# A new order of sparse edge items, panel lists and zeros issued elsewhere, and row additions on TensorE in the first group

## The chip, the cores and the metric

The kernel runs on one core of a Trainium2 chip. Its time is the device time of one execution in microseconds (us); several executions are made, and the median is what counts. One further execution is recorded by the hardware profiler: it gives the page and the trace that are read here.

The engines have short names: PE is TensorE (matrix products; PEld its weight loads), DVE is VectorE, ACT is ScalarE, POOL is GpSimd, SP is SyncE, which here only issues DMA transfers. Each engine works through its own queue of instructions in order.

## The reference

The input x has 32 samples of 512 nodes with 256 features; `adj` is a 512x512 matrix, the same for all samples, with about 1.5% of its entries and the whole diagonal not zero. Four layers follow each other.

```python
def gnn(h, A):                                   # layers 0 and 3
    pre_u, pre_v = h @ W1[:d], h @ W1[d:]
    hidden = relu(pre_u[:, :, None, :] + pre_v[:, None, :, :] + b1)
    S = sigmoid(hidden @ W2 + b2)                # one score for each pair (u, v)
    a = einsum('buv,bud->bvd', S * A, h)
    m = einsum('uv,bud->bvd', A, h) * h
    return beta1 * h + beta2 * (a @ Wa + ba) + beta3 * (m @ Wm + bm)

def layer1(z): return z + relu((A @ z) @ W.T + b)
def layer2(y):                                   # attention over the 512 nodes
    feats = y @ W1.T
    f = feats @ W2 + b2
    return softmax(leaky_relu(f[:, None] + f[None, :]) + A) @ feats + bias2 + y
```

A score S is multiplied by A, so it is needed only where A is not zero.

## The kernel before

**Groups and streams.** The 32 samples are worked in eight groups of four (NB = 4). For each group two "edge groups" exist, g0 for layer 0 and g3 for layer 3. Each of them goes through the same pieces:

- `pre` (L570–L582) computes the rows pre_u and pre_v of all nodes and writes them to a table in DRAM, one row of 1024 values (four samples) for each node and kind;
- `edges` (L611) makes the scores of the entries that are not zero;
- `load` (L727) reads the finished score matrix of four samples back into four tiles called SA, two from each half;
- for layer 0 `middle` follows (layer 0's sums, layers 1 and 2, the `pre` of layer 3), for layer 3 `last` (its sums and the output).

**Items.** An edge group has 36 items of 128 entries each. A node's first eight entries make "own" items (`item_of(c, k)`, eight for each of the four chunks c of 128 nodes); what is left over is packed in four "panels" (`panel_of(half, q)`, two for each half of the nodes). For each item `edges` does this: gather 128 rows of the table by an index list on POOL (`fetch`, L607, an indirect DMA of 512 KB); add the rows `mine` of the other end of the edges (L686, DVE; for an own item these are one contiguous load for each chunk by SP, L647, for a panel another gather by POOL); take relu and multiply by W2 (L694 for all four samples at once, or L702 for one sample with the sum); add up each sample's 256 products on ACT (L672). Four items at a time then go through exp and the sigmoid, and `put` scatters each item's 128 x 4 scores to DRAM (L601, POOL, an indirect DMA). Two DRAM tensors called cells, one for each half (chunks 0 and 1 with the panels of half 0; chunks 2 and 3 with those of half 1), take them. A put waits until the earlier one to the same tensor has landed; `put` therefore takes, from the scores that are ready, one of the half that the last put did not use.

**The order of the items** is the list `order` (L232–L240), the same for all sixteen edge groups. Before, it is four of chunk 0, then three runs of eight that alternate between the chunks 0 and 2, 2 and 1, 1 and 3, and at last the four left of chunk 3 with the four panels between them. So the first four items are all of half 0. In the last eight, six are of half 1 and two, the first two panels, are of half 0.

**Order of instructions.** All these are generators ("streams"). `weave` takes their pieces by given times and issues them in that order; a scheduler then fixes each engine's queue. `behind` keeps edge work on DVE and ACT behind the middle stage's newest piece. Fetches run three items ahead of the additions (LEAD, five in the first g0 and the last g3, LEAD_AT_ENDS). The tiles that they land in are five in rotation, and at the two ends a few more: spare tiles that lie in rooms of the middle stage which are free at that moment (`tags`, `spare`).

**The start.** `setup` and `build` (L249) work out from `adj` which entries there are: for each chunk index list, cell addresses and values; after all four chunks the panels (L345–L380), for which POOL gathers four tiles `got` from a DRAM tensor `lists`. They lie in the rooms h1, hT1, mhT0 and hWa0. The cells of both layers, 2 x 4 MB, are filled with zeros by SP (L538): those of layer 0 by `setup`, those of layer 3 by `zeros_behind`, both from one zero tile in the room hWa3. `middle_before` does for the four samples of the first group what needs no score: it loads the turned sample hT (L816–L820, room hT1, one tile for all four in turn) and makes hWa (hT by Wa, 16 instructions) and mhT (sample by adj, 16 instructions in two pieces, times hT on DVE, L750). The matrix products of `mm` all have line L45. Group 1's `first` (its `pre`) is woven between them.

**The end.** In the last group `last_before` does the same for layer 3, with one hT tile for four samples, and `last_behind` waits for SA and makes the sums (`sums`, L1001 and L1010) and the output.

An fp32 matrix product shows in the trace as two instructions of PE.

## Time and profile before

| what | value |
|---|---|
| median of three executions | 3121.13 us (3118.40, 3121.13, 3138.08) |
| profiled execution | 3102.14 us, of it the span 3100.4 us |
| granted TensorE clock, mean | 0.941 |
| busy: PE, DVE, ACT, POOL | 88%, 74%, 43%, 49% |
| data moved by DMA | 679.40 MB, mean 219 GB/s |
| first matrix product of the first middle stage after its SA landed | 268.22 us |
| last SA tile landed | about 3051 us |

The profiled execution was shorter than the median, so a sum is made against its own time. The span runs from the first to the last instruction; busy time is the share of it in which an engine worked. A wait is put down to the event that ended it: "PE pst L45 <- DMA hT<-xT" is time in which PE stood before a product on line 45 until a transfer into hT had landed. The chain that ended last goes back from the last instruction to what let it start, and so on; a piece of it is on the path that sets the time. A transfer called "SA<-cells" goes from the DRAM tensor cells to the tile SA.

### The profile page before, as it was taken

The page shows a single profiled execution, that of the slowest core. Times are in us where ns is not written, and L with a number is a line of the kernel's source. Part 1 is how long each engine was busy: PE and PEld are TensorE (multiplying, and loading weights), DVE is VectorE, ACT ScalarE, POOL GpSimd, SP SyncE. Part 2 cuts the span into 40 slices and gives each one's busy share as a digit, 9 for nine tenths or more (in the row PEclk, how much of TensorE's full clock was granted, in tenths as well). Part 3 has the DMA queues.
Part 4 walks back from the last instruction along what each step waited for, and adds up shares of the span by engine and source line. Part 5 has one row for each costly group of instructions (what it writes and reads, how often), then busy time and mean ns, then how long its engine had stood idle before and what let it go on. Part 6 is the DMA issues. An engine that isn't in the chain of part 4 may idle for free.

```text
span 3100.4 us, 32465 instructions
## 1 busy us (share of the span) xinstructions
PE 2714.6 (88%) x8645; PEld 1642.5 (53%) x8646; DVE 2302.8 (74%) x6026; ACT 1337.8 (43%) x4101; POOL 1522.5 (49%) x1312
## 2 busy tenths in 40 slices
PE   6366888889998999989998999989999899889957
PEld 3133444446654565546664565545664566545636
DVE  6783886889589875989589885888679795772761
ACT  3453554445345433545354442545335343453440
POOL 1462453556346563556346562565436563450561
PEclk9688988999999999999999999999999999999978
DMA  8874556786677766786668766787568766551753
GB/s 285 282 236 152 180 174 225 237 268 213 223 224 263 235 210 219 247 282 213 227 213 258 238 197 213 242 267 237 188 216 268 251 221 208 178 174 58 234 195 115
DMA packets 302719, 679.40 MB, mean 219 GB/s; under 512 B 52672, under 2 KB 170944, under 8 KB 294336
## 3 DMA queue, kind: packets, MB, share of 16 engines
q0 software_dynamic: 120384, 406.01, 41.0%
q1 hardware_dynamic: 163184, 234.01, 22.5%
q10 hardware_dynamic: 18960, 37.24, 3.2%
q8 instruction: 70, 1.15, 0.2%
q14 instruction: 121, 0.99, 0.1%
HBM read 531.12 MB, written 146.01 MB: 218 GB/s over the span
## 4 chain that ended last, share of the span: by engine, by line
PE 51%; DVE 18%; DMA 17%; issue 6%; ACT 4%; POOL 3%; SPq 0%; POOLq 0%; ACTq 0%; DVEq 0%
PE pst L45 24%; PE pst L1001 7%; DVE rows L686 6%; DMA table<-puv 5%; DMA rows<-table,iv 5%; PE pst L570 3%; DVE rows L702 3%; PE pst L861 3%; PE pst L1010 3%; PE pst L572 3%; DMA cells<-s,cell 3%; DVE rows L694 3%; PE pst L883 2%; PE pst L840 2%; DMA SA<-cells 2%
## 5 line engine op out<-in xcount | busy, mean ns | idle before, releaser
L601 POOL DMA_INDIRECT cells<-s,cell x576 | 691.1, 1200 | 740.7 <-DMA cells<-s,cell 370.3
L607 POOL DMA_INDIRECT rows<-table,iv x554 | 663.3, 1197 | 672.7 <-DMA table<-puv 148.1
L686 DVE TENSOR_TENSOR rows<-rows,mine 128x1024 f32<-128x1024 f32 x554 | 670.8, 1219 | 164.7 <-DMA rows<-table,iv 148.8
L672 ACT ACTIVATE rows<-rows 128x256 f32<-128x256 f32 x1096 | 442.9, 407 | 516.7 <-DVE rows L694 511.1
L45 PE MATMUL pst<-adj,h 128*128 128x512 f32 x1024 | 451.3, 592 | 0.3 <-PE pst L941 0.3
L702 DVE SCALAR_TENSOR_TENSOR rows<-rows,L_gnn_W2bc 128x256 f32<-128x256 f32 x1120 | 415.9, 419 | 1.8
L45 PE MATMUL pst<-L_gnn_Wa,hT 128*128 128x256 f32 x1024 | 264.3, 410 | 118.6 <-DMA hT<-xT 64.6
L694 DVE SCALAR_TENSOR_TENSOR rows<-rows,L_gnn_W2bc 128x1024 f32<-128x1024 f32 x274 | 332.3, 1216 | 0.3
L45 PEld LDWEIGHTS pst<-adj,h 128*128 128x128 f32 x1024 | 192.8, 190 | 222.4 <-issue 218.4
L45 PEld LDWEIGHTS pst<-L_gnn_Wa,hT 128*128 128x128 f32 x1024 | 207.7, 208 | 165.8 <-issue 53.1
L45 PE MATMUL pst<-eT,feats 128*128 128x512 f32 x512 | 231.5, 606 | 12.4 <-ACT eT L953 12.4
L45 PE MATMUL pst<-adjT,zW 128*128 128x512 f32 x512 | 227.8, 597 | 6.2 <-ACT zW L865 6.2
L1001 PEld LDWEIGHTS pst<-hWa,SA 128*128 128x128 f32 x896 | 213.7, 328 | 7.7 <-issue 4.5
L1001 PE MATMUL pst<-hWa,SA 128*128 128x256 f32 x896 | 216.8, 398 | 0.0
L861 PE MATMUL pst<-WT,hT 128*128 128x256 f32 x512 | 150.3, 459 | 75.9 <-DVE hT L848 75.9
L672 ACT ACTIVATION_READ_ACCUMULATOR rows<-rows 128x1 f32 x1096 | 206.7, 189 | 0.0
L809 ACT COPY flat<-SA 128x512 f32<-128x512 f32 x128 | 137.6, 1128 | 155.0 <-PE pst L45 60.1
L840 PE MATMUL pst<-flat,hWa 128*128 128x512 f32 x448 | 196.8, 592 | 0.0
L861 PEld LDWEIGHTS pst<-WT,hT 128*128 128x128 f32 x512 | 118.0, 235 | 114.9 <-DVE hT L848 88.1
L575 ACT COPY puv<-pst 128x256 f32<-128x256 f32 x256 | 93.7, 370 | 183.8 <-DVE puv L574 168.1
L574 DVE TENSOR_TENSOR puv<-pst,bc_L_gnn_b 128x256 f32<-128x256 f32 x256 | 105.0, 416 | 90.3 <-DMA table<-puv 53.8
L45 PEld LDWEIGHTS pst<-eT,feats 128*128 128x128 f32 x512 | 97.5, 193 | 127.5 <-issue 109.8
(170 smaller groups left out, 3979.3 us busy)
## 6 DMA issues: line engine op xcount, KB each, us to landing
table<-puv SPq DMA_DIRECT2D x256, 256.0 KB, 5.5
SA<-cells POOLq DMA_DIRECT2D x64, 1024.0 KB, 7.0
h<-in_x_dram SPq DMA_DIRECT2D x64, 512.0 KB, 6.4
mine<-table SPq DMA_DIRECT2D x64, 512.0 KB, 5.3
hT<-xT SPq DMA_DIRECT2D x36, 512.0 KB, 5.1
h<-x2s SPq DMA_DIRECT2D x36, 512.0 KB, 4.1
xT<-hT ACTq DMA_DIRECT2D x32, 512.0 KB, 5.5
x2T<-yT SPq DMA_DIRECT2D x32, 512.0 KB, 5.3
```

The costliest lines, as they stand in the source:

```text
L45: nc.tensor.matmul(out, lhsT, rhs, start=(n == 0), stop=(n == len(pairs) - 1))
L574: nc.vector.tensor_tensor(puv[:, 0, :], pp[:, 0:D], w["b1bc"], ALU.add)
L601: self.nc.gpsimd.indirect_dma_start(out=g.cells[half], out_offset=bass.IndirectOffsetOnAxis(ap=at, axis=0), in_=s, in_offset=None)
L607: self.nc.gpsimd.indirect_dma_start(out=rows, out_offset=None, in_=g.table, in_offset=bass.IndirectOffsetOnAxis(ap=at, axis=0))
L672: self.behind(nc.scalar.activation(part, part, AF.Identity, accum_out=g.s[:, k, b : b + 1]))
L686: self.behind(nc.vector.tensor_tensor(rows, rows, other, ALU.add))
L694: nc.vector.scalar_tensor_tensor(by_entry, by_entry, 0.0, w2, ALU.max, ALU.mult)
L702: nc.vector.scalar_tensor_tensor(part, part, 0.0, w["W2bc"], ALU.max, ALU.mult, accum_out=at)
L809: self.nc.scalar.copy(flat[:, r, :], SA[r][:, :, b])
L840: nc.tensor.matmul(pz, hWa[:, r, cs], flat[:, r, :], start=(r == 0), stop=False)
L861: nc.tensor.matmul(pw[:, at], zT[:, d, cs], m.WT_1[:, d, :], start=(d + k == 0), stop=(d * k == 1))
L1001: nc.tensor.matmul(pz[:, k * D : (k + 1) * D], SA[r][:, cs, b], hWa[:, r, :], start=(r + k == 0), stop=False)
```

## The change

Six things are edited. Line numbers with "after" are those of the changed kernel.

1. The list `order`: two items of chunk 0; six pairs of chunks 0 and 2; two pairs of chunks 1 and 2; six pairs of chunks 1 and 3, with the panels of half 1 behind the first and the fourth pair; and two pairs, each an item of chunk 3 and a panel of half 0. It holds for all edge groups.
2. In `build` the panel counts and the four gathers into `got` come between the chunks 2 and 1 instead of after all chunks; two of the tiles now lie in the room eT, the others in h1 and hT1. The comparisons that read them stay at the end.
3. `zeros` is issued by POOL instead of SP, for both layers; ahead of those of layer 3, DVE sets the zero tile to zero once more, kept behind the middle stage's newest piece.
4. `edges` has a step `hold` at item 5, which gathers the `mine` rows of the panels early into spare rooms: in the first g0 three of the four (rooms eT for two, mhT3), in the last g3 all four (eT for two, hWa0, mhT0). The spare row tiles of the first g0 are three (yT, mhT0, hWa0) instead of two (yT, mhT3).
5. In the first g0 (`on_pe`) every second item, 18 of 36, has its rows and `mine` added by PE: products with the identity matrix, both into one PSUM tile of 512 columns, twice for an item; relu and W2 are then two DVE operations on 512 columns that read PSUM (after L727) instead of L686 and L694.
6. In `last_before` the hT of the samples 1 to 3 lie in rooms of SA3 tiles instead of in the one hT tile.

Put in the order in which the engines get them, POOL now issues the zeros of layer 0 first, then `got`, then the fetches; before, `got` stood behind the first puts. On PE the products of item 19 stand ahead of the first adj piece of `middle_before` for sample 0, those of 21 between its two adj pieces, those of 23 to 33 ahead of one piece each of the samples 1 to 3, and those of 35 behind all. At the seam from g3 to the next g0 the order on POOL (c30, c31: puts to the halves of layer 3; r0: fetch for layer 0; S30, S31: SA loads) changes like this:

```
before  c31 c30 c31 c30 r0 r0 c30 c31 r0 c30 c31 r0 r0 c31 S30 r0 c31 S30 c31 c31 r0 r0 S31 r0 S31
after   c31 c30 c31 c31 r0 r0 c30 c31 r0 c30 c31 r0 c30 r0 c31 c30 r0 c31 S30 S30 S31 r0 r0 S31 r0
```

```diff
@@ -229,14 +229,19 @@
         self.value = pool.tile([P, ITEMS], F32, name="value")
         self.inode = pool.tile([P, 2 * PANELS], I32, name="inode")
 
-        order = [item_of(0, j) for j in range(OWN // 2)]
-        for lead, other in ((0, 2), (2, 1), (1, 3)):
-            for j in range(OWN // 2):
-                order += [item_of(lead, OWN // 2 + j), item_of(other, j)]
-        tail = [panel_of(h, q) for h in range(2) for q in range(PANELS)]
-        for j in range(OWN // 2):
-            order.append(item_of(3, OWN // 2 + j))
-            order += tail[j : j + 1]
+        ends, most = OWN // 4, OWN - OWN // 4
+        order = [item_of(0, j) for j in range(ends)]
+        for j in range(most):
+            order += [item_of(0, ends + j), item_of(2, j)]
+        for j in range(ends):
+            order += [item_of(1, j), item_of(2, most + j)]
+        for j in range(most):
+            order += [item_of(1, ends + j), item_of(3, j)]
+            if j % (most // PANELS) == 0:
+                order.append(panel_of(1, j // (most // PANELS)))
+        for j in range(ends):
+            order += [item_of(3, most + j), panel_of(0, j)]
+        assert len(order) == len(set(order)) == ITEMS
         self.order = order
 
     def value_of(self, j):
@@ -314,6 +319,36 @@
             yield
         acc, v, there, t = (sheet(NC * OWN) for _ in range(4))
         for c in (0, 2, 1, 3):
+            if c == 1:
+
+                pu = psum()[:, 0 : 2 * PANELS]
+                ones_bf = bf2[:, 1024:1025]
+                nc.vector.memset(ones_bf, 1.0)
+                for k in range(2 * PANELS):
+                    h, q = divmod(k, PANELS)
+                    mm(nc, pu[:, k : k + 1], [(full[:, h * 2 + c, q * P : (q + 1) * P], ones_bf) for c in range(2)])
...
+                inode = self.inode
+                nc.vector.tensor_copy(inode, node)
+                nc.vector.tensor_scalar(self.iu, node, 2.0, None, ALU.mult)
...
+                yield
+                gots = []
+                two = tmp.tile([P, 2, 2 * N], F32, name="got", tag="eT")
+                for k in range(2 * PANELS):
+                    if k < 2:
+                        gots.append(two[:, k, :])
+                    else:
+                        gots.append(tmp.tile([P, 2 * N], F32, name=f"got{k}", tag=("h1", "hT1")[k - 2]))
+                    index = bass.IndirectOffsetOnAxis(ap=inode[:, k : k + 1], axis=0)
+                    nc.gpsimd.indirect_dma_start(out=gots[k], out_offset=None, in_=lists, in_offset=index)
+                yield
             at = slice(c, c + 1)
             js = slice(c * OWN, (c + 1) * OWN)
             target, bias = sheet(OWN), sheet(OWN)
@@ -341,42 +376,16 @@
             nc.vector.tensor_scalar(v[:, js], acc[:, js], 0.5, float(N // 2), ALU.mult, ALU.add)
             self.slots(js, v, there, t, row[:, at], spare)
             yield
-        js = slice(NC * OWN, ITEMS)
...
-        gots = []
-        for k in range(2 * PANELS):
-            gots.append(tmp.tile([P, 2 * N], F32, name=f"got{k}", tag=("h1", "hT1", "mhT0", "hWa0")[k]))
-            index = bass.IndirectOffsetOnAxis(ap=inode[:, k : k + 1], axis=0)
-            nc.gpsimd.indirect_dma_start(out=gots[k], out_offset=None, in_=lists, in_offset=index)
-        yield
         for k in range(2 * PANELS):
             at = slice(k, k + 1)
             rank, adj = gots[k][:, 0:N], gots[k][:, N:]
             junk = bf2[:, 2048 + k % 2 * N :][:, 0:N]
             nc.vector.scalar_tensor_tensor(
-                junk, rank, t[:, at], adj, ALU.is_equal, ALU.mult, accum_out=self.value_of(NC * OWN + k)
+                junk, rank, tp[:, at], adj, ALU.is_equal, ALU.mult, accum_out=self.value_of(NC * OWN + k)
             )
-            nc.vector.scalar_tensor_tensor(junk, rank, slot[:, at], ones, ALU.is_le, ALU.mult, accum_out=v[:, at])
-            yield
-        self.slots(js, v, there, t, start, sp, 0)
+            nc.vector.scalar_tensor_tensor(junk, rank, slot[:, at], ones, ALU.is_le, ALU.mult, accum_out=vp[:, at])
+            yield
+        self.slots(slice(NC * OWN, ITEMS), vp, therep, tp, start, sp, 0)
         yield
 
     def slots(self, js, v, there, t, start, spare, off=None):
@@ -528,6 +537,7 @@
             yield
 
     def zeros_behind(self):
+        self.behind(self.nc.vector.memset(self.zero, 0.0))
         self.zeros(self.cells["3"])
         yield
 
@@ -535,7 +545,7 @@
         for c in cells:
             flat = c[0:CELLS, :].rearrange("(q p a) b -> q p (a b)", q=4, p=P)
             for q in range(4):
-                self.nc.sync.dma_start(flat[q], self.zero)
+                self.nc.gpsimd.dma_start(flat[q], self.zero)
 
     def setup_behind(self):
 
@@ -608,7 +618,9 @@
             out=rows, out_offset=None, in_=g.table, in_offset=bass.IndirectOffsetOnAxis(ap=at, axis=0)
         )
 
-    def edges(self, g, spare=()):
+    def edges(self, g, spare=(), panels=(), on_pe=False):
+
+
 
 
 
@@ -618,7 +630,7 @@
         ready, fetched = [], {}
         lead = LEAD_AT_ENDS if spare else LEAD
         tags = [None] * 5 + list(spare)
-        mine = {}
+        mine, held = {}, {}
         places = g.table.rearrange("(c p k) n -> c k p n", p=P, k=2)
 
         def own_1():
@@ -641,7 +653,9 @@
         def fetch(n):
             j = e.order[n]
             c = j // OWN
-            if c >= NC or c not in mine:
+            if j in held:
+                t = held.pop(j)
+            elif c >= NC or c not in mine:
                 t = self.gath.tile([P, GROUP], F32, name="mine", bufs=3)
                 if c < NC:
                     nc.sync.dma_start(t, places[c, 0])
@@ -657,6 +671,17 @@
             self.fetch(rows, g, e.iv[:, j : j + 1])
             fetched[n] = rows, t
 
+        def hold():
+
+            js = [j for j in e.order if j >= NC * OWN]
+            for tag in panels:
+                n = 2 if tag == "eT" else 1
+                t = self.act.tile([P, n, GROUP], F32, name="held", tag=tag)
+                for k in range(n):
+                    j = js.pop(0)
+                    held[j] = t[:, k, :]
+                    self.fetch(held[j], g, e.iu[:, j - NC * OWN : j - NC * OWN + 1])
+
         def put():
 
             at = next((n for n, r in enumerate(ready) if r[0] != self.half), 0)
@@ -682,8 +707,12 @@
         for k in range(ITEMS):
             for _ in range(2 if spare and len(ready) > 2 else 1):
                 put()
+            if k == LEAD_AT_ENDS:
+                hold()
             rows, other = fetched.pop(k)
-            self.behind(nc.vector.tensor_tensor(rows, rows, other, ALU.add))
+            by_pe = on_pe and k % 2 == 1
+            if not by_pe:
+                self.behind(nc.vector.tensor_tensor(rows, rows, other, ALU.add))
             if k + lead < ITEMS:
                 fetch(k + lead)
             if summed:
@@ -691,7 +720,15 @@
             if spare or k % 2 == 1 and k < ITEMS - 3:
                 by_entry = rows.rearrange("p (b d) -> p b d", b=NB)
                 w2 = w["W2bc"].unsqueeze(1).to_broadcast([P, NB, D])
-                nc.vector.scalar_tensor_tensor(by_entry, by_entry, 0.0, w2, ALU.max, ALU.mult)
+                if by_pe:
+                    for b in range(0, NB, 2):
+                        total, at = self.psum(), slice(b * D, (b + 2) * D)
+                        mm(nc, total, [(self.m.ident, rows[:, at]), (self.m.ident, other[:, at])])
+                        nc.vector.scalar_tensor_tensor(
+                            by_entry[:, b : b + 2, :], by_two(total), 0.0, w2[:, 0:2, :], ALU.max, ALU.mult
+                        )
+                else:
+                    nc.vector.scalar_tensor_tensor(by_entry, by_entry, 0.0, w2, ALU.max, ALU.mult)
                 summed.append(lambda k=k, rows=rows: sums(k, rows))
                 if spare:
                     summed.pop(0)()
@@ -957,8 +994,9 @@
         self.nc.sync.dma_start(h, self.x2s[i])
         return h
 
-    def x2T_of(self, i):
-        hT = self.act.tile([P, DC, N], F32, name="hT3", tag="hT")
+    def x2T_of(self, i, hT=None):
+        if hT is None:
+            hT = self.act.tile([P, DC, N], F32, name="hT3", tag="hT")
         self.nc.sync.dma_start(hT, self.x2T[i])
         return hT
 
@@ -966,7 +1004,8 @@
 
         self.ends = []
         for b in range(NB):
-            h, hT = self.x2_of(i + b), self.x2T_of(i + b)
+            room = self.big(F32, 2048, 3)[:, 0 : DC * N].rearrange("p (c n) -> p c n", c=DC) if b else None
+            h, hT = self.x2_of(i + b), self.x2T_of(i + b, room)
             both = self.big(F32, 2048, 0).rearrange("p (k n) -> p k n", k=2)
             hWa = both[:, 0, :].rearrange("p (c d) -> p c d", c=NC)
             mhT = both[:, 1, :].rearrange("p (c n) -> p c n", c=DC)
@@ -1111,9 +1150,9 @@
             behind = end + 0.29, end + 0.45
         streams += [
             (sp.first(g0, t * NB), first, "fill"),
-            (sp.edges(g0, ("yT", "mhT3") if t == 0 else ()), edges0, ""),
+            (sp.edges(g0, *((("yT", "mhT0", "hWa0"), ("eT", "mhT3"), True) if t == 0 else ())), edges0, ""),
             (sp.middle(g0, g3, t * NB), spread(middle_shares(t == 0), start, end), "main"),
-            (sp.edges(g3, ("yT", "h1", "hT1") if t == last else ()), edges3, "free"),
+            (sp.edges(g3, *((("yT", "h1", "hT1"), ("eT", "hWa0", "mhT0")) if t == last else ())), edges3, "free"),
         ]
         if t == 0:
             streams.append((sp.middle_before(g0, 0), spread(AHEAD, -0.15, -0.03), ""))
```

More of the change, by code (lines that the diff above doesn't have):

```diff
@@ L316, in build @@
         for c in (0, 2, 1, 3):
+            if c == 1:
[5 more added lines that the diff above has]
+                    mm(nc, pu[:, k : k + 1], [(full[:, h * 2 + c, q * P : (q + 1) * P], ones_bf) for c in range(2)])
+                u, node, slot, start, sp, vp, therep, tp = (sheet(2 * PANELS) for _ in range(8))
+                nc.vector.tensor_scalar(u, pu, float(HALF - 1), None, ALU.min)
+                nc.vector.tensor_copy(node, u)
+                nc.vector.tensor_scalar(node[:, PANELS:], u[:, PANELS:], float(HALF), None, ALU.add)
+                inode = self.inode
+                nc.vector.tensor_copy(inode, node)
+                nc.vector.tensor_scalar(self.iu, node, 2.0, None, ALU.mult)
+                nc.gpsimd.iota(slot, [[0, 2], [P, PANELS]], 0, 1, allow_small_or_imprecise_dtypes=True)
+                nc.vector.tensor_scalar(start, u, float(N), None, ALU.mult)
+                nc.vector.tensor_scalar(sp, slot, float(CELLS + NC // 2 * OWN * P), None, ALU.add)
+                nc.vector.tensor_scalar(tp, slot, 1.0, None, ALU.add)
+                yield
[9 more added lines that the diff above has]
+                yield
             at = slice(c, c + 1)
@@ L343, in build @@
             yield
-        js = slice(NC * OWN, ITEMS)
-        pu = psum()[:, 0 : 2 * PANELS]
-        ones_bf = bf2[:, 1024:1025]
-        nc.vector.memset(ones_bf, 1.0)
-        for k in range(2 * PANELS):
-            h, q = divmod(k, PANELS)
-            mm(nc, pu[:, k : k + 1], [(full[:, h * 2 + c, q * P : (q + 1) * P], ones_bf) for c in range(2)])
-        u, node, slot, start, sp, v, there, t = (sheet(2 * PANELS) for _ in range(8))
-        nc.vector.tensor_scalar(u, pu, float(HALF - 1), None, ALU.min)
-        nc.vector.tensor_copy(node, u)
-        nc.vector.tensor_scalar(node[:, PANELS:], u[:, PANELS:], float(HALF), None, ALU.add)
-        inode = self.inode
-        nc.vector.tensor_copy(inode, node)
-        nc.vector.tensor_scalar(self.iu, node, 2.0, None, ALU.mult)
-        nc.gpsimd.iota(slot, [[0, 2], [P, PANELS]], 0, 1, allow_small_or_imprecise_dtypes=True)
-        nc.vector.tensor_scalar(start, u, float(N), None, ALU.mult)
-        nc.vector.tensor_scalar(sp, slot, float(CELLS + NC // 2 * OWN * P), None, ALU.add)
-        nc.vector.tensor_scalar(t, slot, 1.0, None, ALU.add)
-        yield
-        gots = []
-        for k in range(2 * PANELS):
-            gots.append(tmp.tile([P, 2 * N], F32, name=f"got{k}", tag=("h1", "hT1", "mhT0", "hWa0")[k]))
-            index = bass.IndirectOffsetOnAxis(ap=inode[:, k : k + 1], axis=0)
-            nc.gpsimd.indirect_dma_start(out=gots[k], out_offset=None, in_=lists, in_offset=index)
-        yield
         for k in range(2 * PANELS):
```

## The prediction

> **What bounds the kernel now.** First the page: busy time and the costliest groups.
>
> ```profile
> PE 2714.6 (88%) x8645; PEld 1642.5 (53%) x8646; DVE 2302.8 (74%) x6026; ACT 1337.8 (43%) x4101; POOL 1522.5 (49%) x1312
> ...
> L601 POOL DMA_INDIRECT cells<-s,cell x576 | 691.1, 1200 | 740.7 <-DMA cells<-s,cell 370.3
> L607 POOL DMA_INDIRECT rows<-table,iv x554 | 663.3, 1197 | 672.7 <-DMA table<-puv 148.1
> L686 DVE TENSOR_TENSOR rows<-rows,mine 128x1024 f32<-128x1024 f32 x554 | 670.8, 1219 | 164.7 <-DMA rows<-table,iv 148.8
> ```
>
> TensorE is busy 88% of the span, so it is nearly the bound; what an edit can win lies in the other 12%. Every put (L601) and every fetch (L607) holds POOL 1.2 us, and puts to one half wait for each other: 370.3 us of POOL's idle time is that. Next, where TensorE's idle time lies: busy time by stretches (start in three pieces, first middle stage, the steady groups, the end).
>
> ```profile
> 140.00:200.00 60.00, 24.77 (x70) 15.39 (x71) 52.15 (x94) 30.61 (x135) 41.35 (x32) 0.68 0.72 236
> 200.00:268.00 68.00, 38.92 (x97) 20.30 (x95) 29.45 (x55) 24.83 (x98) 36.97 (x35) 0.84 0.77 266
> 268.00:482.00 214.00, 178.48 (x509) 95.36 (x510) 152.59 (x405) 105.60 (x279) 85.70 (x75) 0.88 0.48 152
> 482.00:2880.00 2398.00, 2235.81 (x7178) 1348.27 (x7177) 1858.32 (x5030) 1045.96 (x3080) 1217.63 (x1040) 0.97 0.69 223
> ```
>
> The columns are PE, PEld, DVE, ACT, POOL, granted clock, DMA share, GB/s. Steady groups: PE 2235.8 of 2398, 93%. From 140 to 268 it is 64 of 128, at a clock of 0.68 and 0.84, while DVE has 52 of the first 60. What PE waits for there, in the waits of 0 to 268:
>
> ```profile
> PE pst L45 <- DMA hT<-xT: 64.6, 3, 37.3
> ...
> DVE big L374 <- DMA got<-lists,inode: 16.0, 1, 16.0
> ```
>
> and the chain that ended last, of that stage (start, length, what):
>
> ```profile
> 138.15 4.26 DMA got<-lists,inode
> ...
> 149.31 7.20 DMA hT<-xT
> ...
> 254.72 6.84 DMA cells<-s,cell
> 262.08 4.98 DMA SA<-cells
> 267.08 1.10 ACT flat L809
> 268.22 2.08 PE pst L840 x2
> ```
>
> So the first middle stage starts at 268.22, behind the last puts and the SA load of the first group. Two strands lead there: POOL and DVE (fetch, add, put), and PE's four rounds of middle_before, each behind a load into the one hT tile (149.31, 185.64, 209.22, 235.49), the last done at 252.4. Then the waits from 400 to 2700:
>
> ```profile
> POOL cells L601 <- DMA cells<-s,cell: 309.0, 137, 6.1
> ...
> DVE rows L686 <- DMA rows<-table,iv: 117.5, 42, 8.8
> ...
> PE pst L861 <- DVE hT L848: 71.1, 18, 8.5
> ```
>
> The third is what the first costs at the seams g3→g0: fetches stand on POOL behind puts of one half in a row (1003.75, 1010.08, 1016.35, 1021.70), rows come late, DVE stops for up to 8.8 us, and L848, queued behind the add, holds PE. Last, the end of the chain:
>
> ```profile
> 3028.96 12.12 PE pst L45 x32
> 3041.07 0.46 PE pst L1001 x2
> 3041.53 0.44 issue
> 3041.98 0.56 POOL SA L727
> 3042.54 8.43 DMA SA<-cells
> 3051.02 8.57 PE pst L1001 x26
> ```
>
> The last SA tile lands at 3051, behind half-1 puts at 3027.20, 3030.50, 3035.32 and 3039.33; after it 49 us of sums remain.
>
> **The start (lists, spare rooms, TensorE's adds).** *Lists.* The four list gathers no longer stand behind the first puts on POOL, and their adds lie before chunks 1 and 3 of the build. DVE's 16.0 us at 142.44 go. What is late next: the first rounds of fetches. Fetches begin at 83.13, a put and a fetch take 1.2 + 0.3 us each, and 36 + 36 + 4 of them are 114 us; POOL could be through at 197 and is at 258, so it isn't POOL's rate but the round DVE–ACT–put. DVE has 52.15 of 60 us in 140–200. The 16 us count at most once, as the earlier first hT load: the got tiles hold h1 and hT1 until about 149. I take 7 of them (0 to 16), so a first load at 142: SP's loads of that moment and the build's own DVE work stay in front.
> *Held panel rows, three spare row tiles.* Four panel fetches move ahead of item 10's (4 × 1.5 = 6 us of POOL, same count); one more row tile lets a fetch start earlier. I cost both at nothing while DVE, 52 of 60 us busy, is behind the fetches; if that cover goes, 6 us either way, inside the bounds below.
> *Adds on TensorE.* 18 odd items leave an add (L686, pitch 1.14 us) and a 128x1024 product (L694, 1.14) and get two 128x512 products out of PSUM; no such row exists, nearest are L750 and L930, 0.60 us at a pitch: 18 × (2.28 − 1.20) = 19 us off DVE. PE gets 18 × 4 fp32 matmuls of 128x512. Nearest row: L45 with adj, eight in 6.87–7.03 us, 0.86 each: 72 × 0.86 = 62 us. Upper end: a row from behind a wait, L45 on hT at 156.64, takes 3.75 us for what takes 1.89 at 163.42, so every group that starts cold takes up to twice as long: 62 to 124. PE has 13.2 + 9.2 + 24.8 + 38.9 = 86 us of the 188 from 80 to 268; it has room for 62, not for 124.
> But the items' matmuls stand in PE's in-order queue between the pieces of middle_before (items 19, 21, 23 … 33 each ahead of one piece, 35 after all). An item whose rows are late holds the next round, and what is queued behind it is group 1's pre and the hT of the next sample. A round is then: hT load 7, PE's own hWa (16 instructions, 3.45–5.24) and adj (16, 7.03), two items 6.9, pre 2.6, and the turn over DVE's L750: about 29 us, where it was 36, 24 and 26. From a load at 142, 4 × 29 = 116: PE ends at 258 instead of 252.4. Item 35 still has product (1.2), sums (1.7), sigmoid (2), put (1.2, landing 3–5) and SA load (5–7) behind it, about 15–20 us. SA at 273–278 against 267, +8.
> *Zeros out of the window.* 4 MB of the 8 MB of zeros leave the stretch 40–110, which runs at 325–390 GB/s with DMA full (share 0.91–1.02): 4 MB at 390 GB/s is 10.8 us of DMA; part of it was filling gaps, so −4 (−8 to 0).
> Sum of the start: +8 for PE's rounds, less 4, less 2 for DVE's lighter queue: **+2** (−20, if the whole 16 us and 4 of the zeros count; +20, if the items start cold).
>
> The Trainium skill, "TensorE: Matmul & The Clock Gate", section "What's actually happening", says the clock has two states, half and full, and that some 3.4 us of work set it full. The 3.75 against 1.89 us above is such a factor of two. By it the items would partly pay for themselves: in the 37, 19, 8 and 9 us in which PE waits for hT they keep the clock up, and the hWa groups of four rounds would take 3.45 instead of 5.24 us, 7 us in all.
>
> **Zeros for layer 3.** They go from SP's queue to POOL's, behind a DVE memset inside the first middle stage. POOL: 8 issues at 0.57 (L727's row) + 0.3 = 7 us, ahead of the first c00 puts and fetches; 4 MB of DMA at 390 GB/s is 11 us, where DMA share is 0.48. SP loses eight issues that hold it 12.93 us at 23.86, where the zeros for layer 0 move to POOL too, and are out earlier. DVE's memset of 128x1024 about 1 us. Cover: PE has 178.5 of 214 in that stretch and edge work is not late until the g0→g3 seam. **+3** (0 to +8, all of it if the fetches behind them are late).
> The Trainium skill, "DMA: Bandwidth & Descriptors", section "Issuing engine by pattern", gives simple loads and stores to SyncE, and says POOL's path is the slower. By its first-byte figures, 1 us against 0.6, eight issues in a row would be 0.4 us later; the trace's own landing times (7.3 us median for zeros from SP) don't tell the paths apart.
>
> **The order of items, steady groups.** At the seam g3→g0 the old end is eight items of half 1 with the panels; now the last eight alternate halves. POOL's order there holds two half-1 puts fewer in series ahead of the r0 fetches, but one SA load of half 1 (which waits for the last put) moves ahead of three of them. Two puts are 2 × 5 us off each seam; the SA wait takes about 5 back on half of the fetches. Seven seams have 117.5/7 = 17 us of DVE waits each and 71.1/7 = 10 of PE. If a seam gives PE 1.5 us, seven give 10: **−10** (−40, over half of the 71.1; +10, if the SA wait holds the fetches). At the seam g0→g3 the c00 put moves behind half 1, S00 with it; nothing there waits over 3 us.
>
> **The end.** The two early panel rows and the last puts alternate halves: of the four half-1 puts 3.3–5.0 us apart, two become half-0 puts which overlap. Held panel rows remove `mine<-table,iu` at 3004.48, 8.06 us in the chain, but its fetch joins an earlier POOL queue. hT rooms take 19.6 + 15.0 + 6.2 us of PE waits on x2T off a strand that ends at 3041, before SA; they hide behind SA, and new: three SA3 tiles wait until those rooms are read. −10 (−18, the half-1 puts and the panel's 8 us both; −3, only one put): **−10**.
>
> **Sum.** +2 + 3 − 10 − 10 = −15 on the profiled execution's 3102.14 (span 3100.4, 2 us around it). That execution is 19 us below the median of 3121.13; I put the difference on the median: **3106**. Low ends: −20 + 0 − 40 − 18 = −78; high ends: +20 + 8 + 10 − 3 = +35. 1%, 31 us, is about what a measurement of this kernel (3118 to 3138) tells from no change.
>
> **Rivals.**
> *The seams pay in full (0.25).* For it: PE's 71.1 us at seams come from one cause, and the got stall of 16 us is a plain wait. Start −12, zeros +2, seams −30, end −13: −53, 3068. Against: POOL's waits move to the SA load.
> *TensorE's queue holds the start (0.22), slower.* One mechanism: middle_before's hT loads stand behind items whose rows are late. It decides once an item's wait is longer than PE's idle time in that round (8–9 us in the last two). Three items late by 7 us: start +22, zeros +5, seams 0, end −5: +22, 3143; with cold items (+20 more) 3163.
> *Nothing moves (0.08).* The puts' landing times set seams and end in any order: 3121.
> The forecast itself 0.45, 3088 to 3120.
>
> Faster by over 1%: the first rival but its weak third, and the forecast's low edge: 0.17 + 0.09 = 0.26. Slower by over 1%: half of the second: 0.12. Within 1%: 0.62. The range leaves out the far half of each outer rival: 3062 to 3148.
>
> **What the profile after would show.** Right: no DVE wait on got; the first hT load at 140–145; DVE waits on PE at the new product; first L840 at 265–280; DVE's waits on rows between 400 and 2700 below 90 us and PE's on L848 below 60; last SA tile 8–12 us earlier against the end. Wrong, if the first L840 comes after 285 or before 250, if the seams' waits stay at 117 and 71, or if SA's load at the end waits for PE's reads of the rooms.

## The result, and the profile after

The changed kernel takes 3182.34 us (median of four executions, 3179.11 to 3184.80), the kernel before beside it 3128.21 us (3118.40 to 3138.08): a ratio of 1.017, with a 95% interval of 1.015 to 1.019. It is 54 us slower. The forecast was 3106 us, 15 us faster, with a range up to 3148: sign and range were both wrong.

One caution about the profiles. The profiled execution of the kernel before took 3102.14 us, while none of its timed executions in the studies below was under 3114; their medians were 3128 to 3132. The two profiled spans differ by 3177.2 − 3100.4 = 77 us, the medians by 54. So some 23 us of what the two traces show, most of it in the steady groups, belongs to that one quick execution. Sizes below come from medians; traces are used for where and why.

From the page of the changed kernel, its busy times and the lines that answer to those shown of before:

```profile
PE 2788.7 (88%) x8789; PEld 1669.3 (53%) x8790; DVE 2286.9 (72%) x6027; ACT 1338.6 (42%) x4101; POOL 1529.1 (48%) x1328
...
L611 POOL DMA_INDIRECT cells<-s,cell x576 | 696.5, 1209 | 708.3 <-DVE s L648 298.0
L617 POOL DMA_INDIRECT rows<-table,iv x552 | 664.9, 1204 | 719.5 <-DMA table<-puv 277.4
L715 DVE TENSOR_TENSOR rows<-rows,mine 128x1024 f32<-128x1024 f32 x537 | 648.3, 1217 | 242.6 <-DMA rows<-table,iv 193.9
```

What was to be moved is moved: PE is busy 74 us longer, DVE 16 us shorter, and DVE has 17 additions fewer in the trace. But the wait of the puts now ends at DVE (L648 makes the scores), no longer at the put before; and DVE's idle time ahead of the additions rose from 164.7 to 242.6 us.

Busy time by stretches (PE, PEld, DVE, ACT, POOL, granted clock, DMA share, GB/s), with the start up to the first middle stage, that stage, and the steady groups:

```profile
140.00:200.00 60.00, 41.87 (x109) 22.67 (x108) 36.80 (x66) 30.81 (x138) 33.46 (x29) 0.83 0.71 234
200.00:284.90 84.90, 54.22 (x130) 27.21 (x128) 19.55 (x49) 18.86 (x68) 22.77 (x25) 0.83 0.42 129
284.90:509.00 224.10, 185.33 (x515) 97.58 (x516) 153.46 (x406) 107.74 (x280) 88.91 (x83) 0.86 0.53 173
509.00:2972.00 2463.00, 2248.18 (x7175) 1349.44 (x7174) 1857.11 (x5028) 1043.92 (x3078) 1225.22 (x1040) 0.96 0.68 217
```

In the second stretch no engine is near its limit: PE 54 of 85, DVE 20, POOL 23, DMA share 0.42. The start is now a chain of waits between engines. The steady stretch has nearly the same PE work as before (2248 us against 2236) in a longer time (2463 us against 2398).

Where the time went can be dated by the first score product (L840, after it L877) of each sample in the timeline. Sample 1 of the first group came at 320.3 and now at 341.4, 21 us later; the last of the 32 samples at 2818.6 and now at 2911.2, 92.6 later; from there to the end of the span it is 281.8 and now 266.0, 16 less. So in the traces: start +21, steady groups +72, end −16.

The waits from 0 to 300 (engine, line, releaser, total, times, longest) show the start's new waits, which stood at 64.6 and 16.0 for hT and got:

```profile
PE pst L45 <- DMA hT<-xT: 32.4, 4, 10.9
DVE rows_more L727 <- PE pst L45: 17.8, 7, 13.4
...
PE pst L877 <- ACT flat L846: 16.4, 1, 16.4
```

The DVE wait on got is gone, and PE waits half as long for hT. In their place DVE waits for TensorE's adds, and at the end PE stands 16.4 us before the first score product.

The waits of the steady groups, first before (490 to 2860):

```profile
POOL cells L601 <- DMA cells<-s,cell: 307.3, 135, 6.1
DVE rows L686 <- DMA rows<-table,iv: 121.9, 43, 8.8
...
PE pst L861 <- DVE hT L848: 75.3, 20, 8.5
```

and after, same limits:

```profile
POOL cells L611 <- DMA cells<-s,cell: 224.0, 120, 5.5
DVE rows L715 <- DMA rows<-table,iv: 159.2, 44, 10.4
...
PE pst L898 <- DVE hT L885: 99.4, 20, 12.3
DVE rows L715 <- DMA mine<-table,iu: 48.1, 12, 7.4
...
PE pst L884 <- DVE mhT L787: 20.8, 5, 5.4
PE pst L582 <- DVE yT L967: 17.6, 6, 3.3
```

The new order did what it was read to do: puts wait 83 us less for the put before them. Yet the rows come no earlier, and three waits appear that did not exist: DVE on a panel's `mine` row (before: 2.4 us), and PE behind DVE at two places where DVE stood on that row.

### The profile page after: what moved, and what is told of

The parts are those of the page before. It is cut to its first block, busy times and chain, and to the rows that moved or that the text cites. A ratio compares the mean times of both kernels' runs of the same rounds, so it can differ in the third digit from the quotient of the medians.

```text
span 3177.2 us, 32832 instructions
## 1 busy us (share of the span) xinstructions
PE 2788.7 (88%) x8789; PEld 1669.3 (53%) x8790; DVE 2286.9 (72%) x6027; ACT 1338.6 (42%) x4101; POOL 1529.1 (48%) x1328
## 5 line engine op out<-in xcount | busy, mean ns | idle before, releaser
L715 DVE TENSOR_TENSOR rows<-rows,mine 128x1024 f32<-128x1024 f32 x537 | 648.3, 1217 | 242.6 <-DMA rows<-table,iv 193.9
L731 DVE SCALAR_TENSOR_TENSOR rows<-rows,L_gnn_W2bc 128x1024 f32<-128x1024 f32 x262 | 317.5, 1213 | 0.4
L45 PE MATMUL pst<-L_gnn_Wa,hT 128*128 128x256 f32 x976 | 243.3, 399 | 35.4 <-DMA hT<-xT 32.4
L45 PEld LDWEIGHTS pst<-L_gnn_Wa,hT 128*128 128x128 f32 x976 | 191.9, 202 | 77.0 <-issue 41.2
L877 PE MATMUL pst<-flat,hWa 128*128 128x512 f32 x448 | 196.8, 592 | 0.0
```

The source lines that it names most:

```text
L45: nc.tensor.matmul(out, lhsT, rhs, start=(n == 0), stop=(n == len(pairs) - 1))
L715: self.behind(nc.vector.tensor_tensor(rows, rows, other, ALU.add))
L731: nc.vector.scalar_tensor_tensor(by_entry, by_entry, 0.0, w2, ALU.max, ALU.mult)
L877: nc.tensor.matmul(pz, hWa[:, r, cs], flat[:, r, :], start=(r == 0), stop=False)
```

## The experiments

Each kernel is named in words; "sample 1" is its first score product in the first middle stage (320.3 before, 341.4 after). Medians are set against 3182 for the changed kernel and against the kernel before of the same study, which was 3131.7, 3128.3, 3129.0 and 3128.8.

### The order of before in the changed kernel

```diff
-        ends, most = OWN // 4, OWN - OWN // 4
...
+        order = [item_of(0, j) for j in range(OWN // 2)]
+        for lead, other in ((0, 2), (2, 1), (1, 3)):
...
```

> The changed kernel with the item order of before; all else as changed. Theory A, the new order costs the 65 us that the seven steady groups lost in the traces (the first product of the last group's last sample came 92.6 us later, that of the first middle stage's second sample 21.1 us later): the time falls by 55 to 70 us from the changed kernel's 3182, to 3112-3127, and DVE's waits on panel rows (48.1 us, 12 times) go. Theory B, the order is innocent and the later start or the zeros drag through the groups: the time stays above 3165.

Measured: 3139.29 us, 1.0021 of before (0.9999 to 1.0043). The order costs 43 us, somewhat less than the 55 to 70 that were expected from the traces; the quick profiled execution of the kernel before would explain why the traces promised more. Sample 1 stays at 340.5: the order has no part in the loss of the start. DVE's waits on panel rows fall to 3.5 us.

### The new order alone in the kernel before

```diff
-        order = [item_of(0, j) for j in range(OWN // 2)]
...
+        ends, most = OWN // 4, OWN - OWN // 4
+        order = [item_of(0, j) for j in range(ends)]
...
```

> The kernel before with the new item order alone. Theory A: 50 to 70 us slower than before, 3178-3198, with the start (first product of the first middle stage) within 8 us of 268 and the loss in the steady groups. Theory B: within 15 us of before.

Measured: 3169.92 us, 1.012 (1.0092 to 1.0149), 38 us slower than before; sample 1 at 321.8. Again the order, again less than the traces promised. From the last sample to the end of the span it is 279.0 us, in the next kernel, which has the chunk order of before, 277.2: for the end of this kernel the order brings nothing that can be seen.

### The early panels alone

```diff
-        tail = [panel_of(h, q) for h in range(2) for q in range(PANELS)]
         for j in range(OWN // 2):
             order.append(item_of(3, OWN // 2 + j))
-            order += tail[j : j + 1]
+            if j < PANELS:
+                order.append(panel_of(0, j))
+        for q, at in ((0, 20), (1, 27)):
+            order.insert(at, panel_of(1, q))
```

> The kernel before with its own order of chunks, but the two panels of half 1 put at the positions 20 and 27, where the new order has them. Theory A1, it is the two panels in the middle of the stream, whose second gather stands three items ahead only: 40 to 65 us slower than before, with DVE waits on panel rows near 48 us. Theory A2, it is the order of chunks (six pairs instead of four, halves alternating at the end): less than 15 us slower.

Measured: 3132.65 us, 1.0014 (0.9994 to 1.0034). A1 falls as it stood: with the old order of chunks the same panels at the same positions cost nothing, and DVE waits 0.6 us on their rows. A2 was not thereby shown; the next kernels part the two. This profile (span 3128.4) also serves as a usual execution of the kernel before: its last sample comes 32.6 us later than in the quick one.

### The new chunk order, panels at the end

```diff
-            if j % (most // PANELS) == 0:
-                order.append(panel_of(1, j // (most // PANELS)))
         for j in range(ends):
             order += [item_of(3, most + j), panel_of(0, j)]
+        order += [panel_of(1, q) for q in range(PANELS)]
```

> The changed kernel with its new order of chunks, but both panels of half 1 moved from the positions 20 and 27 to the end. Theory A3, the order costs only where its chunks and the early panels meet: the panel at 20 comes one item after chunk 3's first and three after chunk 2's last, so that its gather waits on POOL for a mine tile (34.3 us in all behind DVE's adds, against 18.2 with the order of before) and DVE then waits for it (48.1 us): these waits go to below 20 and below 5 us, and the time falls by 30 to 45 us from 3182, to 3137-3152, as with the order of before. Theory A4, it is the order of chunks and the alternating end at the seam: 3170-3185.

Measured: 3152.72 us (3131.75 to 3166.43), 1.0067 (1.0038 to 1.0095). 30 of the 43 us come back, just outside the stated 3152. POOL's waits of panel gathers for DVE's adds fall to 1.2 us as expected, DVE's waits on panel rows only to 32.1, since four panels in the last five items are now gathered close together. So the cost lies mostly where the new chunk order and the early panels meet.

### One early panel two positions later

```diff
-            if j % (most // PANELS) == 0:
-                order.append(panel_of(1, j // (most // PANELS)))
+            if j in (1, 3):
+                order.append(panel_of(1, (1, 3).index(j)))
```

> The changed kernel with its new order, but the first panel of half 1 two positions later (22 instead of 20; the second stays at 27). Theory A5, the room: between the items 19 and 31 chunks 1 and 3 hold two of the three mine tiles, and the third is free from item 17's add on, so a panel's gather that POOL has to issue right then waits; at 22 it waits no more: POOL's waits of mine gathers for DVE's adds fall from 34.3 to below 20 us, DVE's waits on panel rows from 48 to below 25, and the time is 3150-3168. Theory A6, any panel in the middle of this order costs the same: 3175-3190, the waits as they were.

Measured: 3142.82 us, 1.0041 (1.0022 to 1.0059): 40 us less than the changed kernel, for moving one item of 36 by two places. That is more than A5 promised (3150–3168), and A6 falls. POOL's waits of panel gathers for DVE's adds fall from 34.3 to 4.6 us. Of the waits from 490 to 2860 no line on `mine` is left for DVE, of PE's for L787's mhT one of 0.4 us, and of those for L967's yT only the short ones at L580 that were there before:

```profile
POOL cells L611 <- DMA cells<-s,cell: 239.8, 109, 6.2
DVE rows L715 <- DMA rows<-table,iv: 202.0, 57, 9.4
...
PE pst L898 <- DVE hT L885: 121.4, 21, 13.5
```

What remains are DVE's waits on ordinary rows: 202.0 us here (this profile is of the longest of its executions, 3161.38 us), 140 to 169 in the other four traces with the new order, 122 to 175 in the three with the chunk order of before told so far. They differ from trace to trace by more than the two orders differ. What happens at the early panels is seen in the changed kernel's timeline of POOL (start, length, operation, idle time before it and its releaser) and of DVE:

```profile
959.53 0.97 POOL L617 DMA_INDIRECT mine<-table,iu  x1 [0.30 <-issue]
...
962.11 0.95 POOL L617 DMA_INDIRECT rows<-table,iv  x1 [0.31 <-issue]
967.74 0.94 POOL L617 DMA_INDIRECT mine<-table,iu  x1 [4.67 <-DVE rows L715]
971.78 1.69 POOL L617 DMA_INDIRECT rows<-table,iv  x1 [3.10 <-DVE rows L739]
```

```profile
966.24 1.23 DVE L715 TENSOR_TENSOR rows<-rows,mine 128x1024 f32<-128x1024 f32 x1 [4.54 <-DMA mine<-table,iu]
```

The first gather is issued at 959.53, and DVE needs its row before it lands at 966.24: a wait of 4.54. Meanwhile the second gather stands on POOL until an addition on DVE is done, and every put and fetch behind it stands too (4.67, then 3.10). DVE's mhT product is queued behind that addition, and PE waits 4.09 us for it (L884 at 973.38). Twelve waits of DVE on a panel's row, one in each edge group from 664 us on but the last, make up the 48.1 us; behind five of them POOL's second gather stands 2.5 to 6.0 us, behind six 1.6 to 2.3.

The two gathers are those of the two panels of half 1, and the second starts only 8.2 us behind the first, one row fetch between them, though its item comes seven places later. With the first panel two places later they lie 18.6 us apart, four row fetches between them, and neither waits:

```profile
959.48 0.99 POOL L617 DMA_INDIRECT mine<-table,iu  x1 [0.30 <-issue]
...
978.10 1.17 POOL L617 DMA_INDIRECT mine<-table,iu  x1 [0.30 <-DVE hT L885]
```

That two chunks hold two of the three `mine` tiles there, so that only one is left for panels, is read from the code and fits all four kernels; a fourth tile was not tried, so this reason for the waits is argued and not shown.

### No adds on TensorE, with the new order

```diff
-            (sp.edges(g0, *((("yT", "mhT0", "hWa0"), ("eT", "mhT3"), True) if t == 0 else ())), edges0, ""),
+            (sp.edges(g0, *((("yT", "mhT0", "hWa0"), ("eT", "mhT3"), False) if t == 0 else ())), edges0, ""),
```

> The changed kernel without the adds on TensorE: DVE does all 36 items of the first group. Theory C, items 21 to 35 stand behind the hT loads in TensorE's queue and so their puts and the SA load come late (SA waited 16.4 us after TensorE's last item): the first middle stage starts 10 to 20 us earlier than 284.9, and the time is 10 to 20 us shorter, 3162-3172. Rival: DVE's 19 us of work are missed and the start is the same or later, 3180-3195.

Measured: 3140.88 us, 1.0024 (1.0006 to 1.0042): 41 us less, twice what was expected. Sample 1 comes at 307.8 instead of 341.4, 33.6 us earlier and 12.5 earlier than before the change.

### Neither the new order nor the adds

The edits of the first kernel and of the one just told, together.

> The changed kernel with the order of before and without the adds on TensorE; lists, zeros, held rows and rooms of the end as changed. If the two costs add up (43 us for the order, 41 for the adds on TensorE): 3093-3105, which is 0.8 to 1.2% faster than the kernel before, from the start's lists and the end's rooms. If both had one cause: 3130-3145, no gain from taking both away.

Measured: 3104.60 us (3101.41 to 3106.32), 0.9922 of before (0.9893 to 0.9951). Taken away singly the order gave 43 us and the adds 41, taken away together 78: the two costs nearly add up. What is left of the change makes the kernel 24 us faster than before.

### TensorE adds only the early items

```diff
-            by_pe = on_pe and k % 2 == 1
+            by_pe = on_pe and k % 2 == 1 and k < 20
```

(with the order of before)

> The order of before, and TensorE adds only the odd items up to 19, that is those ahead of the rounds of hT loads in its queue. If an item costs only where it stands behind those loads (theory C): the first middle stage starts as early as without any adds on TensorE or up to 10 us earlier, since DVE is spared 10 of its 19 us; 3085-3105. If every add on TensorE costs: 3110-3125.

Measured: 3105.45 us (3088.64 to 3117.67), 0.991 (0.988 to 0.9941), and sample 1 at 304.7, 3.9 us earlier than without any. Ten items on TensorE cost nothing, and what they bring doesn't show in the time.

### TensorE adds only the late items

```diff
-            by_pe = on_pe and k % 2 == 1
+            by_pe = on_pe and k % 2 == 1 and k >= 20
```

(with the order of before)

> The order of before, all else as changed, and TensorE adds only the odd items from 21 on (eight of them), those that its queue holds between the rounds of hT loads. Theory C, place: nearly the whole cost of the adds is here; the first product of the first middle stage's second sample comes 25 to 33 us later than the 308.6 without adds on TensorE, and the time is 3130-3142, against 3104.6. Rival, number: eight of eighteen items cost eight eighteenths, 12-16 us; 3116-3122.

Measured: 3139.28 us, 1.0039 (1.0014 to 1.0064), and sample 1 at 346.5, 38 us later than without. Eight items cost as much as all eighteen (3139.29): it is their place, not their number. Two things happen there. First, the rounds get longer. The next hT load waits for the last product that reads the one hT tile, and the items' products stand between. From the first of the four hT loads to PE's last product it was this without adds on TensorE, 144.12 to 239.63, 95.5 us:

```profile
144.12 0.34 SPq L852 DMA_DIRECT2D hT<-xT  x1
...
232.60 7.03 PE L45 MATMUL pst<-adj,h 128*128 128x512 f32 x16
```

and with the eight late items, 143.84 to 273.92, 130.1 us:

```profile
143.84 0.34 SPq L852 DMA_DIRECT2D hT<-xT  x1
...
272.90 1.02 PE L45 MATMUL pst<-mine,ident 128*128 128x512 f32 x2
```

Of the 34.6 us between the two, the items' own 32 products of 0.86 us make up 27.5, by estimate. Second, the items wait for the rounds' loads. That is to be seen in the changed kernel's timelines of PE, DVE and POOL around the last rounds:

```profile
245.32 3.75 PE L45 MATMUL pst<-L_gnn_Wa,hT 128*128 128x256 f32 x8 [8.05 <-DMA hT<-xT]
248.87 1.61 PE L45 MATMUL pst<-rows_more,ident 128*128 128x512 f32 x2
```

```profile
251.38 0.69 DVE L727 SCALAR_TENSOR_TENSOR rows_more<-pst,L_gnn_W2bc 128x512 f32<-128x512 f32 x1 [13.38 <-PE pst L45]
```

```profile
235.34 0.97 POOL L617 DMA_INDIRECT rows<-table,iv  x1 [0.30 <-issue]
256.05 1.00 POOL L611 DMA_INDIRECT cells<-s,cell  x1 [19.74 <-DVE s L648]
```

PE waits 8.05 us for hT; only behind that and the hWa products come the item's adds. DVE, in order, stands 13.38 us before the item's product, and POOL stands 19.74 us before a put whose score is not made (20.57 in the round before), with its fetches queued behind. Two odd items pass in each round of about 30 us, and behind the last one PE waits 16.4 us more for the SA tiles.

### Zeros on SP again

```diff
-                self.nc.gpsimd.dma_start(flat[q], self.zero)
+                self.nc.sync.dma_start(flat[q], self.zero)
```

(order of before, no adds on TensorE)

> The order of before, no adds on TensorE, and the zeros of both layers issued by SP again. If the zeros' move brings the start: the start is 5 to 10 us later and the time 3110-3116. If it costs in the first middle stage (5 to 6 us between its second and third sample's first products): 3096-3101. If neither, within 4 us of 3104.6.

Measured: 3106.06 us, 0.9923 (0.99 to 0.9946), against 3104.60: no difference clear of the spread. Sample 1 comes 1.7 us earlier.

### One hT tile at the end again

```diff
-            room = self.big(F32, 2048, 3)[:, 0 : DC * N].rearrange("p (c n) -> p c n", c=DC) if b else None
+            room = self.big(F32, 2048, 3)[:, 0 : DC * N].rearrange("p (c n) -> p c n", c=DC) if False else None
```

(order of before, no adds on TensorE)

> The order of before, no adds on TensorE, and the hT of the last group's samples 1 to 3 again in the one hT tile. If those loads stood behind SA at the end anyway (as argued before the result): within 4 us of 3104.6, with TensorE's waits on hT<-x2T back near 44 us. If the rooms are what the end gained: 6 to 12 us slower, 3110-3117.

Measured: 3113.96 us, 0.9949 (0.9927 to 0.9972): 9.4 us slower than with the rooms, and 7.9 slower than the kernel with the zeros on SP (3106.06), which has the rooms as well. From the last sample to the end of the span it is 279.2 us, with the rooms 270.6. PE's waits at the end, without the rooms and then with them:

```profile
PE pst L45 <- DMA hT<-x2T: 27.9, 3, 18.3
PE pst L45 <- ACT rows L692: 11.5, 1, 11.5
PE pst L1035 <- DMA SA<-cells: 9.8, 2, 8.6
```

```profile
PE pst L1035 <- DMA SA<-cells: 35.0, 2, 28.7
PE pst L45 <- DMA h<-x2s: 5.2, 1, 5.2
```

All of the first two lines stood ahead of hWa products, which read hT; the waits on hT<-x2T are 27.9 us, not the 44 expected. These 39.4 us go, and 25.2 of waits for SA and 5.2 for h come: part of the strand was on the path.

### The lists alone in the kernel before

The edit is the second of the change, the block of panel counts and gathers ahead of chunk 1 with the new rooms of its tiles, and nothing else.

> The kernel before with the panel lists alone moved. If the start's gain of 12 us comes from the lists: the first middle stage's second sample starts 8 to 14 us earlier than 320.3, and the time is 3115-3122 (before: 3128-3132). If the freed DVE wait on the lists (16.0 us) only turns into another wait: within 4 us of before.

Measured: 3113.33 us, 0.9949 (0.9927 to 0.9971): 15.7 us faster than before, with sample 1 at 305.4, 14.9 us earlier, both a little more than expected. As much as DVE's wait on the lists (16.0 us) is gone from the time. The first hT load came 8.3 us earlier (141.04 against 149.31). The rest came in the first round, which shrank from 36.3 to 25.5 us. In the kernel before, the mhT product that frees the hT tile stood behind edge work on DVE until 184.93; here it ran at 165.84.

## Why the prediction was wrong

From the medians the change reads like this: order +43, adds on TensorE +35, lists −16, rooms at the end −9, zeros 0. That makes +53; 54 were measured. Each was measured in one surrounding only and is known to some 8 us (the intervals of the ratios are 0.4 to 0.6% wide). The held panel rows and the third spare row tile were not tried apart. The forecast had a term for each, and the two that decide were wrong in sign or size.

**Adds on TensorE: the start at +2, measured +17 at the first product behind SA (284.92 against 268.22) and +21 at sample 1.** The room on PE and DVE was sized rightly: 62 us of matmuls on an engine with 100 idle. The step that failed is the sum of the rounds, 4 × 29 from a first load at 142, PE's end at 258. The first load came at 138.93, but the rounds took 38, 31 and 30 us (next loads at 177.04, 208.06 and 238.03) and the last one, to PE's end, 30, so PE ended at 268.5. The first score product came 16.4 us behind it, as the sum had it (15 to 20). The 4 and 2 us that were taken off for zeros and DVE's lighter queue do not show.

A comparison was also missing. PE's end was set against the 252.4 of before, but with the lists alone it is 236.0, and sample 1 comes at 305.4. So the sum hid most of what the adds cost behind what the lists brought. Before the change the items hardly depended on the rounds: DVE added them, and in all it stood 14.7 us before PE's mhT products. Tied into PE's queue, the last items could finish no earlier than a last round that they themselves put off. The rival of TensorE's queue named the right queue with another mechanism: PE waited for an item's rows only once, 12.2 us up to 90.31, ahead of the rounds. The rounds were put off by the items' products, and the items by the rounds' loads.

**Lists: 7 of 16 us taken, 15.7 measured.** The first hT load moved by 8.3 us, as taken. What was missing is the round behind it, 10.8 us shorter: the build's own DVE work and the busy DVE (52 of 60 us) were named as what stays in front, but in the kernel before, DVE's edge work held up the mhT product of that round, and with the lists moved it did not.

**The seams: −10, measured +43 for the order.** The puts' serial waits fell as read, from 307.3 to 224.0 us, and were worth nothing: with the panel two places later they are 239.8 us, with the order of before 340.0, and the times are 3142.82 and 3139.29. So the reading that these waits make the rows late and hold PE doesn't hold; rows came no earlier. What was missing is a term: the order moves the panels, and each panel needs a second gather on POOL and a `mine` tile of its own. The working counted puts and SA loads at the seam and never looked at `fetch` for a panel in the middle of the stream, though its 8.06 us at the end stood in the chain of before. So the bound of +10 was drawn from the seam alone. The forecast's own signs say so too: DVE's waits on rows and PE's on L848's hT were to fall below 90 and 60 us and rose to 159.2 and 99.4 (490 to 2860).

**Zeros: −4 in the window and +3 in the first middle stage; measured 0 together.** The sum was right within what could be measured; the two parts were not measured apart.

**The end: −10, measured −16 in the traces.** In sum within its bounds (−18 to −3), but not by the terms that were given, and so by luck. The alternating puts, which were to bring it, bring nothing that shows in the kernel before (279.0 us from the last sample to the end, against 277.2 to 284.4 in the three traces with its chunk order). In the changed one it is 265 to 266 us in the four traces with the new order and 270 to 274 in the five with the old order and the rooms, some 5 us less. The rooms, costed at nothing because they hide behind SA, bring 9.4 us. The new wait of SA for them (rows of SA on POOL) was below 2 us in the traces, but for one of 3.8 with the panels late.

**The basis.** The sum was made on one profiled execution that was quicker than all later ones of that kernel. It moved no sign; its DVE waits on rows (121.9 us from 490 to 2860) were the lowest of all traces with that chunk order (131 to 175 in the others).

Version for use: the change without the new order and without the adds on TensorE takes 3104.60 us, 0.9922 of before; with TensorE adding the items up to 19 it is 3105.45 and not to be told from it.

## What to carry to other kernels

Before work is handed to an engine with idle time, ask what it will stand behind in that engine's queue: idle time that consists of waits is no room for work that must be ready before those waits end, and work put between a load and the last reader of its tile puts off the next load too. Ten items ahead of the loads cost nothing, eight among them 35 us. When items of a stream are reordered, count for each kind of item all that it fetches and each rotating tile it holds while it is in flight; one panel two places too early cost most of 43 us, while the puts for which the order was changed lost 83 us of waiting without any effect on the time.

## What the runs showed of the hardware

TensorE is slower behind waits of some us (granted clock 0.83 from 140 to 284.9, 0.96 in the steady groups). After waits of 7.21, 10.91, 6.25 and 8.05 us for hT the first eight hWa instructions took 3.75 us each time, the next eight 1.89. After a wait of 1.13 us four instructions of L580 (at 74.40) took 1.98 us, against 1.88 without a wait. The Trainium skill, "TensorE: Matmul & The Clock Gate", section "What's actually happening", gives an idle window of some 3.4 us after which the clock is halved; the four long waits and the short one agree. The items' matmuls did not keep the clock up there, as they stood behind the waits.

Moving 8 MB of plain writes from SP's queue to POOL's made no difference in the time (3104.60 against 3106.06 us). The Trainium skill, "DMA: Bandwidth & Descriptors", section "Issuing engine by pattern", gives such writes to SyncE; no cost of the other choice could be measured here.

Ten or more executions of the same kernel spread by 20 to 35 us (the kernel before, 33 executions of one study: 3115.23 to 3142.84), and a profile is one execution. Its trace shows where waits are; a difference of two traces below that spread shows no size.
